# Expert weights inside the activations: the third feed-forward of a four-layer kernel, groups 1 to 3

## The chip, the cores and the metric

The kernel runs on one core of a Trainium2 chip. The metric is the device time of one execution in microseconds (us). Three runs of the kernel before took 1149.76, 1147.95 and 1148.5 us, so the median is 1148.5 us.

The core has engines that work side by side, each with its own queue that is worked off in order: TensorE (PE in the profile, with PEld for its weight loads), VectorE (DVE), ScalarE (ACT), GpSimd (POOL), and SyncE (SP), which here does nothing but issue DMAs.

## The reference

Four layers, each a cross-attention over 77 context positions and a feed-forward, run over 2 x 1024 tokens of width 256, all in fp32. The part that matters is the feed-forward of the third layer, a mixture of eight experts:

```
x = x + ffn(layernorm(x))

logits = xn @ gate_weight.T                  # 8 experts
scores = sigmoid(logits)
choice = scores + bias                       # pairs of experts form 4 groups:
                                             # keep the 2 groups with the largest sums,
                                             # then the 2 experts with the largest choice
w      = scores of the 2 experts kept, divided by (their sum + 1e-20)
y[t]   = sum over kept experts e of
         w[t, e] * ( silu(xn[t] @ gate_e.T) * (xn[t] @ up_e.T) ) @ down_e.T
```

A weight that multiplies a whole token's row can be applied to the expert's output (256 numbers) or to its hidden activations (128 numbers) alike, since the down projection is linear.

## The kernel before

The 2048 tokens lie in SBUF as four groups (`g`) of four sub-tiles (`j`) of 128 tokens. All eight experts are computed for every token; an expert that isn't chosen has weight 0.

The third feed-forward is `layer2_ffn` (L700 to L770; layers count from 0). It has three pieces:

- `route(g)` (L709 to L734) normalizes a group, transposes it to `xnT` (feature on the partition), makes the router's logits on TensorE, and on DVE the sigmoid, the choice of groups and experts (`top_mask`, L206 to L216, which compares every pair of values) and the weights `cw`, a tile of 128 tokens x 4 sub-tiles x 8 experts.
- `hidden(g, e)` (L736 to L751) makes one expert's hidden activations for the group's 512 tokens: four matmuls of 128x512 (L745) into two PSUM banks `pgu`, Silu on ACT (L750), the product with the up half on DVE (L751). The result `hT` has the expert's 128 hidden features on the partitions and tokens along the free axis.
- `down(g, j)` (L753 to L768) makes, for one sub-tile, eight matmuls of 128x256 (L758), each expert into its own quarter of two PSUM tiles `po`, and then eight multiply-adds on DVE (L765), `x = po * cw[:, j, e] + x`. Here tokens lie on the partitions, so the weight is one number per partition.

PSUM tiles come from helpers: `pbig` (L81, two tiles of two banks, used by `pgu`, by `po` and by most large products), `pone` (L86, one bank, three tiles in turn), `pside` (L94, one bank).

The driver (L1374 to L1416) works one group after the other: eight `hidden`, then four `down`. Between the pieces it puts work of other layers: the pieces of `chain` (the second layer's feed-forward and the third layer's attention, L554 to L690, for group g + 2), pieces of the last layer's set-up (`setup`, L795 to L882: products `pw` at L870, written to DRAM as `vd`), and `route(g + 1)`. Before that, `beside` (L1379) runs the chain of groups 0 and 1 next to the second layer's attention.

The written order isn't what the engines run: the framework's planner (switched on at L1489) simulates the program, reorders the instructions of each engine by its own estimates, and fixes the queues before the run.

After the stage comes `layer3_attention` (L884): it takes the SBUF that the closed pools leave, loads rope tables `cs` (L888), values `vw` (L897) and, for every sub-tile, a bias `rb` (L920, 616 KB), to which POOL adds a mask (L924), and makes queries `pq` on TensorE (L930) that DVE and POOL rotate (L781 to L791).

Of the kernel before, what the change touches and what calls it, by code (L numbers as in the profile page):

```python
# [22 lines left out]
F32 = mybir.dt.float32  # L23
# [4 lines left out]
AF = mybir.ActivationFunctionType  # L28
ALU = mybir.AluOpType
# [4 lines left out]
P = 128  # L34
D = 256
KC = D // P
NB, S = 2, 1024
NT = NB * S
G, J = 4, 4
GT = P * J  # L40
# [3 lines left out]
E = 8  # L44
CAP = 320
HID = 1024
INTER = 128
# [19 lines left out]
def tile_layers(ctx: ExitStack, tc: tile.TileContext, a: dict, out: bass.AP):  # L67
    nc = tc.nc
# [5 lines left out]
    st = ctx.enter_context(tc.tile_pool(name="st", bufs=3))  # L74
# [3 lines left out]
    dp = ctx.enter_context(tc.tile_pool(name="dram", bufs=1, space=DRAM))  # L78
    ps2 = ctx.enter_context(tc.tile_pool(name="ps2", bufs=2, space=PSUM))

    def pbig(name):  # L81
        return ps2.tile([P, 2, 512], F32, tag="p2", name=name)
# [3 lines left out]
    def pone(name):  # L86
        turn[0] += 1
        pool, tag = ((ps1, "p1"), (pst, "pt"))[turn[0] % 2]
        return pool.tile([P, 512], F32, tag=tag, name=name)
# [4 lines left out]
    def pside(name):  # L94
        return psr.tile([P, 512], F32, tag="pr", name=name)
# [7 lines left out]
    ident = cst[:, C_ID : C_ID + P]  # L103

    tokens = [xp.tile([P, J, ROW], F32, name=f"x{g}") for g in range(G)]
    xs = [t[:, :, :D] for t in tokens]
# [21 lines left out]
    def rowvec(name, n=D, parts=P):  # L128

        t = cp.tile([parts, n], F32, name=f"r_{name}")  # L130
        nc.sync.dma_start(t, a[name].partition_broadcast(parts))
        return t

    def weight(shape, name):
        return wp.tile(shape, F32, tag="w", name=name)
# [95 lines left out]
    def bc(v, n):  # L231

        return v.unsqueeze(len(v.shape)).to_broadcast([*v.shape, n])
# [62 lines left out]
    def attention(lay, weights, mask, deep=5, beside=None):  # L296
# [4 lines left out]
        with tc.tile_pool(name=f"at_{lay}", bufs=2) as ap:  # L301
# [175 lines left out]
            if beside:  # L477
                stages.append(beside)
# [210 lines left out]

        return prepare, scores, weighed, weights_turned, values, add  # L690

    def layer2_ffn_weights():
        wgu = []
        for nm in ("gate2T", "up2T"):
            t = weight([P, KC, E * INTER], nm)
            nc.sync.dma_start(t, a[nm].rearrange("(c p) n -> p c n", p=P))
            wgu.append(t)
        return wgu

    def layer2_ffn(fp, wgu):  # L700

        wd = weight([P, E, D], "down2T")
        nc.sync.dma_start(wd, a["down2T"].rearrange("e i h -> i e h"))
        gw = cp.tile([P, KC, E], F32, name="gw2")
        nc.sync.dma_start(gw, a["router2T"].rearrange("(c p) e -> p c e", p=P))
        gb = rowvec("L2_ffn_e_score_correction_bias", E)
        xnTs, cws, hTs = {}, {}, {}

        def route(g):  # L709
            n = f"f2{g}"  # L710
            xnTs[g] = xnT = normed(g, n, "f2")
            pl = small_logits(xnT, gw, n)

            sc = st.tile([P, J, E], F32, tag="sc", name=f"sc_{n}")
            nc.scalar.activation(sc, pl, AF.Exp, scale=-1.0)
            nc.vector.tensor_scalar(sc, sc, 1.0, None, ALU.add)
            nc.vector.reciprocal(sc, sc)
            ch = st.tile([P, J, E], F32, tag="ch", name=f"ch_{n}")
            nc.vector.tensor_tensor(
                ch, sc, gb.unsqueeze(1).to_broadcast([P, J, E]), ALU.add  # L720
            )
            pairs = ch.rearrange("p j (q i) -> p j q i", i=2)
            gs = st.tile([P, J, 4], F32, tag="gs", name=f"gs_{n}")
            nc.vector.tensor_tensor(gs, pairs[:, :, :, 0], pairs[:, :, :, 1], ALU.add)
            gm = top_mask(gs, 4, 2, f"{n}g")
            nc.vector.tensor_tensor(pairs, pairs, bc(gm, 2), ALU.mult)
            keep = top_mask(ch, E, 2, n)
            cws[g] = cw = st.tile([P, J, E], F32, tag="cw", name=f"cw_{n}")
            nc.vector.tensor_tensor(cw, sc, keep, ALU.mult)
            tot = st.tile([P, J], F32, tag="tot", name=f"tot_{n}")  # L730
            nc.vector.tensor_reduce(tot, cw, AX.X, ALU.add)
            nc.vector.tensor_scalar(tot, tot, 1e-20, None, ALU.add)
            nc.vector.reciprocal(tot, tot)
            nc.vector.tensor_tensor(cw, cw, bc(tot, E), ALU.mult)  # L734

        def hidden(g, e):  # L736
            n = f"f2{g}"
            if e % 4 == 0:
                hTs[g, e // 4] = fp.tile(
                    [P, E // 2, GT], F32, tag="hT", name=f"hT_{n}{e}", bufs=3  # L740
                )
            pgu = pbig(f"pgu_{n}{e}")
            for i in range(2):
                for kc in range(KC):
                    nc.tensor.matmul(  # L745
                        pgu[:, i, :], wgu[i][:, kc, e * INTER : (e + 1) * INTER],
                        xnTs[g][:, kc, :], start=(kc == 0), stop=(kc == KC - 1),
                    )
            sg = fp.tile([P, GT], F32, tag="sg", name=f"sg_{n}{e}")
            nc.scalar.activation(sg, pgu[:, 0, :], AF.Silu)  # L750
            nc.vector.tensor_tensor(hTs[g, e // 4][:, e % 4, :], sg, pgu[:, 1, :], ALU.mult)  # L751

        def down(g, j):  # L753
            x = xs[g][:, j, :]
            for half in range(2):
                po = pbig(f"po_f2{g}{j}{half}")
                for e in range(4):
                    nc.tensor.matmul(  # L758
                        po[:, e // 2, (e % 2) * D : (e % 2) * D + D],
                        hTs[g, half][:, e, j * P : (j + 1) * P], wd[:, 4 * half + e, :],  # L760
                        start=True, stop=True,
                    )
                for e in range(4):
                    ee = 4 * half + e
                    nc.vector.scalar_tensor_tensor(  # L765
                        x, po[:, e // 2, (e % 2) * D : (e % 2) * D + D],
                        cws[g][:, j, ee : ee + 1], x, ALU.mult, ALU.add,
                    )  # L768

        return route, hidden, down  # L770


    KV = 4
# [586 lines left out]
    with tc.tile_pool(name="masks", bufs=1) as mp:  # L1360
        mask0 = mp.tile([P, G, J * L], a["mask0"].dtype, name="mask0")
        mask1, mask2 = (
            mp.tile([P, G, J * L], a[f"mask{i}"].dtype, tag="mask", name=f"mask{i}")
            for i in (1, 2)
        )
        mb0, mb1 = (
            mp.tile([P, G, J * L], BF16, tag="mb", name=f"mb{i}") for i in range(2)
        )
        ctxn = mp.tile([L, NB, D], F32, name="ctxn")
        nc.sync.dma_start(ctxn, a["ctxn"].rearrange("b k d -> k b d"))  # L1370
        layer0_attention()
        with tc.tile_pool(name="none", bufs=1) as np0:
            layer0_ffn(np0)
        with (  # L1374
            tc.tile_pool(name="q8", bufs=1) as qp, tc.tile_pool(name="a2", bufs=1) as ap2,
        ):
            chain = []

            def beside(it):  # L1379


                if it == 0:
                    chain.extend((*layer1_ffn(qp, *quantized), *layer2_attention(ctxn, ap2)))
                for g in range(2):
                    k = it - (g + 1) * J + 1
                    if 0 <= k < len(chain):
                        chain[k](g)

            weights = attention_weights(
                "a1", ["L1_xattn_wq", "L1_xattn_wk", "L1_xattn_wv", "L1_xattn_wo"],  # L1390
                "L1_xattn_bo",
            )
            setup = layer3_setup()
            next(setup)
            quantized = layer1_ffn_setup()
            next(setup)
            gate_up = layer2_ffn_weights()
            layer1_attention(weights, beside)
            with tc.tile_pool(name="a3s", bufs=2) as sp, tc.tile_pool(name="f2", bufs=2) as fp:
                route, hidden, down = layer2_ffn(fp, gate_up)  # L1400
                setup.send(sp)


                route(0)
                for g in range(G):
                    pieces = [lambda e=e: hidden(g, e) for e in range(E)]
                    pieces += [lambda j=j: down(g, j) for j in range(J)]
                    for k, piece in enumerate(pieces):
                        if g + 2 < G and k < len(chain):
                            chain[k](g + 2)  # L1410
                        piece()
                        if g < 2 and k % 2 == 1 and k > 4 or (g, k) in ((0, 1), (0, 3)):
                            next(setup)
                        if g + 1 < G and k == E:
                            route(g + 1)
                made3 = next(setup)  # L1416
    route, experts = layer3_ffn()
# [75 lines left out]
```

## Time and profile before

| | |
|---|---|
| median of three runs | 1148.5 us |
| the profiled execution | 1150.59 us |
| its span (first to last instruction) | 1148.7 us |
| TensorE busy | 1029.8 us (90%) |
| VectorE busy | 719.4 us (63%) |
| GpSimd busy | 386.3 us (34%) |
| ScalarE busy | 362.1 us (32%) |
| mean granted TensorE clock | 0.952 |
| the chain that ended last | PE 56%, DVE 24%, DMA 7%, ACT 4%, issue 4%, POOL 4% |

A row of a group of instructions reads: source line, engine, operation, output <- inputs, shapes, how often | busy us, mean ns of one | idle us of that engine just before them, and what ended most of it. So a row with a high mean tells what a thing costs, and the part after the second bar tells whether its engine had to stand still for it. A row of the timeline reads: start us, length us, engine, line, operation, with idle time in square brackets. TensorE's matmuls are pipelined, so lengths of groups of them overlap a little.

Four gate and up matmuls with their four partners (one expert) take 3.43 us of TensorE, the eight down matmuls of one sub-tile 1.73 us when nothing holds them; one DVE multiply-add takes 0.48 us.

### The profile page before, as it was taken

The page shows a single profiled execution, that of the slowest core. Times are in us where ns is not written, and L with a number is a line of the kernel's source. Part 1 is how long each engine was busy: PE and PEld are TensorE (multiplying, and loading weights), DVE is VectorE, ACT ScalarE, POOL GpSimd, SP SyncE. Part 2 cuts the span into 40 slices and gives each one's busy share as a digit, 9 for nine tenths or more (in the row PEclk, how much of TensorE's full clock was granted, in tenths as well). Part 3 has the DMA queues.
Part 4 walks back from the last instruction along what each step waited for, and adds up shares of the span by engine and source line. Part 5 has one row for each costly group of instructions (what it writes and reads, how often), then busy time and mean ns, then how long its engine had stood idle before and what let it go on. Part 6 is the DMA issues. An engine that isn't in the chain of part 4 may idle for free.

```text
span 1148.7 us, 13916 instructions
## 1 busy us (share of the span) xinstructions
PE 1029.8 (90%) x4770; PEld 645.5 (56%) x4770; DVE 719.4 (63%) x1848; ACT 362.1 (32%) x1115; POOL 386.3 (34%) x368
## 2 busy tenths in 40 slices
PE   5499999999998987897998999899899958999996
PEld 3255554444444444455655546577678844766774
DVE  5567965776578898949586547677878731222211
ACT  1457640000076563131231110555355521111100
POOL 5443320112343544423120000675566641121211
PEclk9699998999999898898999999999999987999998
DMA  8400008245200000111102004523042323253630
GB/s 269 57 3 1 1 23 165 38 82 88 80 1 1 1 1 1 39 48 31 40 23 59 1 1 161 145 45 67 23 103 51 90 83 96 77 165 101 200 131 17
DMA packets 100279, 74.89 MB, mean 65 GB/s; under 512 B 57916, under 2 KB 90476, under 8 KB 100206
## 3 DMA queue, kind: packets, MB, share of 16 engines
q1 hardware_dynamic: 92974, 58.20, 18.3%
q10 hardware_dynamic: 4800, 9.46, 4.8%
q0 software_dynamic: 2432, 6.31, 1.6%
q8 instruction: 40, 0.66, 0.2%
q14 instruction: 33, 0.27, 0.1%
HBM read 55.35 MB, written 19.64 MB: 65 GB/s over the span
## 4 chain that ended last, share of the span: by engine, by line
PE 56%; DVE 24%; DMA 7%; ACT 4%; issue 4%; POOL 4%; SPq 0%; POOLq 0%; DVEq 0%; ACTq 0%
PE pe_f L545 10%; PE pgu_f L745 8%; PE poe_e L1273 4%; PE ph_e L1253 4%; PE po_a L1007 4%; DMA out_x<-ye_e,ids_e 3%; PE pq_a L930 3%; DVE x L765 3%; PE pc_a L450 3%; DVE x L156 2%; PE po_f L758 2%; PE pPT_a L437 2%; DVE mx_a L410 2%; DMA xe_e<-buf 2%; DVE sm_a L417 2%
## 5 line engine op out<-in xcount | busy, mean ns | idle before, releaser
L412 ACT ACTIVATE s_a<-psc_a,mx_a 128x77 f32<-128x77 f32 x512 | 121.5, 337 | 58.5 <-DVE mx_a L410 52.1
L419 POOL TENSOR_TENSOR s_a<-s_a,sm_a 128x616 f32<-128x616 f32 x64 | 78.3, 1223 | 123.9 <-DVE sm_a L418 89.4
L545 PE MATMUL pe_f<-ew,xnT_f 128*128 128x512 f32 x256 | 117.1, 607 | 0.0
L551 DVE SCALAR_TENSOR_TENSOR x<-pe_f,gate_f,x 128x256 f32<-128x256 f32 x128 | 61.8, 483 | 43.3 <-PE pe_f L545 40.7
L981 ACT ACTIVATE s_a<-s_a,mx_a 128x77 f32<-128x77 f32 x256 | 67.2, 347 | 61.4 <-DVE mx_a L979 61.2
L545 PEld LDWEIGHTS pe_f<-ew,xnT_f 128*128 128x128 f32 x256 | 48.3, 195 | 55.0 <-issue 53.0
L1007 PE MATMUL po_a<-vw,PT_a 128*128 128x256 f32 (+1 forms) x320 | 77.3, 381 | 0.8 <-ACT PT_a L1002 0.8
L1253 PE MATMUL ph_e<-xT_e,w 128*128 128x320 f32 x256 | 75.6, 436 | 0.0
L758 PE MATMUL po_f<-down2T,hT_f 128*128 128x256 f32 x256 | 65.0, 400 | 8.8 <-DVE x L765 8.7
L437 PE MATMUL pPT_a<-cst,s_a 128*128 128x128 f32 (+1 forms) x320 | 55.0, 292 | 17.8 <-POOL vr_a L343 11.5
L410 DVE TENSOR_REDUCE mx_a<-psc_a 128x4 f32<-128x308 f32 x128 | 57.9, 466 | 18.6 <-PE psc_a L401 11.4
L1077 DVE TENSOR_SCALAR hT_e<-ph_e,b1c 128x320 f32<-128x320 f32 (+1 forms) x36 | 20.6, 572 | 75.3 <-PE ph_e L1253 75.3
L930 PE MATMUL pq_a<-wq,xnT_a 128*128 128x512 f32 x128 | 60.5, 610 | 4.7 <-DVE s_a L972 4.7
L745 PE MATMUL pgu_f<-xnT_f,gate2T 128*128 128x512 f32 x128 | 63.5, 619 | 1.0 <-DVE hT_f L751 0.6
L765 DVE SCALAR_TENSOR_TENSOR x<-po_f,cw_f,x 128x256 f32<-128x256 f32 x128 | 60.8, 480 | 5.7 <-PE po_f L758 2.5
L437 PEld LDWEIGHTS pPT_a<-cst,s_a 128*128 128x128 f32 (+1 forms) x320 | 35.9, 143 | 49.5 <-issue 17.9
L1007 PEld LDWEIGHTS po_a<-vw,PT_a 128*128 128x128 f32 (+1 forms) x320 | 57.8, 190 | 9.6 <-issue 1.4
L1075 ACT ACTIVATE hT_e<-ph_e,b1c 128x320 f32<-128x320 f32 (+1 forms) x36 | 19.6, 545 | 138.0 <-PE ph_e L1253 138.0
L1273 PE MATMUL poe_e<-w,hT_e 128*128 128x256 f32 x256 | 61.3, 381 | 0.0
L758 PEld LDWEIGHTS po_f<-down2T,hT_f 128*128 128x128 f32 x256 | 48.3, 197 | 22.7 <-DVE x L765 15.4
L450 PE MATMUL pc_a<-PT_a,vblk_a 128*32 128x256 f32 (+1 forms) x512 | 57.2, 400 | 4.2 <-DVE PT_a L445 2.2
L745 PE MATMUL pgu_f<-xnT_f,up2T 128*128 128x512 f32 x128 | 60.1, 592 | 0.0
(311 smaller groups left out, 1979.8 us busy)
## 6 DMA issues: line engine op xcount, KB each, us to landing
w<-in_L_ffn_w SPq DMA_DIRECT2D x16, 1024.0 KB
rb_a<-in_relbias SPq DMA_DIRECT2D x16, 616.0 KB
buf<-none ACTq DMA_DIRECT2D x12, 769.5 KB
vd<-vo SPq DMA_DIRECT2D x8, 308.0 KB
vw<-vd SPq DMA_DIRECT2D x2, 1152.0 KB
xe_e<-buf SPq DMA_DIRECT2D x8, 257.0 KB
x<-in_x SPq DMA_DIRECT2D x4, 512.0 KB
ew<-in_L_ffn_expert_w SPq DMA_DIRECT2D x4, 512.0 KB
```

The lines of the kernel that those rows point to most:

```text
L410: nc.vector.tensor_reduce(mx, sv, AX.X, ALU.min)
L412: nc.scalar.activation(s[:, c, 4 * i + h, :], sv[:, h, :], AF.Exp, bias=mx[:, h : h + 1], scale=-1.0,)
L437: nc.tensor.transpose(pt[: wide(m), m - m0, k * P : (k + 1) * P], sp[k][:, c, m * P : m * P + wide(m)], ident,)
L450: nc.tensor.matmul(pc[cols, c, :], vblk[g // 2][: wide(m), c, m, cols], t[: wide(m), m, :], start=(k == 0), stop=(k == 1),)
L545: nc.tensor.matmul(pe[:, i, :], xnT[:, kc, j * P : (j + 1) * P], ew[half][:, kc, i * 512 : (i + 1) * 512], start=(kc == 0), stop=(kc == KC ...
L745: nc.tensor.matmul(pgu[:, i, :], wgu[i][:, kc, e * INTER : (e + 1) * INTER], xnTs[g][:, kc, :], start=(kc == 0), stop=(kc == KC - 1),)
L758: nc.tensor.matmul(po[:, e // 2, (e % 2) * D : (e % 2) * D + D], hTs[g, half][:, e, j * P : (j + 1) * P], wd[:, 4 * half + e, :], start=Tr ...
L765: nc.vector.scalar_tensor_tensor(x, po[:, e // 2, (e % 2) * D : (e % 2) * D + D], cws[g][:, j, ee : ee + 1], x, ALU.mult, ALU.add,)
L930: nc.tensor.matmul(pq[:, i, :], xnTs[g][:, kc, j * P : (j + 1) * P], wq[:, kc, i * 512 : (i + 1) * 512], start=(kc == 0), stop=(kc == KC - 1),
L1007: nc.tensor.matmul(po, t[:w, m, :], vws[g // 2][:w, m, :], start=(m == 0), stop=(m == NC3 - 1))
L1253: nc.tensor.matmul(ph[:, h % 2, :rows], w1[:, kc, h * P : (h + 1) * P], xT[:, kc, :], start=(kc == 0), stop=(kc == KC - 1),)
L1273: nc.tensor.matmul(po, hT[:, h, i * P : (i + 1) * P], w2[:, h, :], start=(h == 0), stop=(h == NH - 1),)
```

## The change

For groups 1 to 3 the weights are applied to the hidden activations instead of to the outputs. There the features lie on the partitions, so a weight has to be the same on all 128 partitions and differ along the free axis. `route(g)` therefore transposes `cw` (four transposes on TensorE into one `pside` tile, a copy on ACT) and writes the 8 x 512 numbers to DRAM (16 KB). `hidden(g, 0)` reads them back in eight DMAs, one per expert, each spreading one row of 512 numbers over all 128 partitions (256 KB, tag `cb`, eight buffers). In `hidden`, POOL multiplies Silu's result by `cb` before DVE multiplies it with the up half. In `down`, the eight matmuls of a sub-tile add up in one PSUM bank (`pone` instead of `pbig`), and one DVE add brings the sum to x. Group 0 keeps the old way.

So that the weights of the router are at hand earlier, `layer2_ffn()` is called before the second layer's attention, and `route(0)` stands at the end of `beside` instead of ahead of the group loop. `hidden` and `down` come from `units(fp)`, inside the pool.

The edits to `route`, `hidden` and `down`, and the driver:

```diff
-            cws[g] = cw = st.tile([P, J, E], F32, tag="cw", name=f"cw_{n}")
+            cw = st.tile([P, J, E], F32, tag="cw", name=f"cw_{n}")
...
             nc.vector.tensor_tensor(cw, cw, bc(tot, E), ALU.mult)
+            if g == 0:
+                cws[g] = cw
+                return
+
+            pc = pside(f"pcw_{n}")[:E, :]
+            for j in range(J):
+                nc.tensor.transpose(pc[:, j * P : (j + 1) * P], cw[:, j, :], ident)
+            cwT = st.tile([E, J, P], F32, tag="gT", name=f"cwT_{n}", bufs=2)
+            cwT = cwT.rearrange("e j p -> e (j p)")
+            nc.scalar.copy(cwT, pc)
+            cwds[g] = cwd = dp.tile([E, GT], F32, name=f"cwd_{n}")
+            nc.sync.dma_start(cwd, cwT)
...
+            def hidden(g, e):
+                n = f"f2{g}"
+                if e == 0 and g > 0:
+                    for i in range(E):
+                        cbs[i] = fp.tile([P, GT], F32, tag="cb", name=f"cb_{n}{i}", bufs=8)
+                        nc.sync.dma_start(cbs[i], cwds[g][i, :].partition_broadcast(P))
...
+                nc.scalar.activation(sg, pgu[:, 0, :], AF.Silu)
+                if g > 0:
+                    nc.gpsimd.tensor_tensor(sg, sg, cbs[e], ALU.mult)
+                nc.vector.tensor_tensor(hTs[g, e // 4][:, e % 4, :], sg, pgu[:, 1, :], ALU.mult)
...
+                po = pone(f"po_f2{g}{j}")[:, :D]
+                for e in range(E):
                     nc.tensor.matmul(
-                        pgu[:, i, :], wgu[i][:, kc, e * INTER : (e + 1) * INTER],
-                        xnTs[g][:, kc, :], start=(kc == 0), stop=(kc == KC - 1),
+                        po, hTs[g, e // 4][:, e % 4, j * P : (j + 1) * P], wd[:, e, :],
+                        start=(e == 0), stop=(e == E - 1),
                     )
...
+                nc.vector.tensor_tensor(x, x, po, ALU.add)
...
+                if it == J + len(chain):
+                    route(0)
...
-            gate_up = layer2_ffn_weights()
+            route, units = layer2_ffn()
             layer1_attention(weights, beside)
             with tc.tile_pool(name="a3s", bufs=2) as sp, tc.tile_pool(name="f2", bufs=2) as fp:
-                route, hidden, down = layer2_ffn(fp, gate_up)
+                hidden, down = units(fp)
                 setup.send(sp)
 
 
-                route(0)
                 for g in range(G):
```

More of the change, by code (lines that the diff above doesn't have):

```diff
@@ L690, in layer2_attention, with layer2_ffn @@
         return prepare, scores, weighed, weights_turned, values, add
-    def layer2_ffn_weights():
+    def layer2_ffn():
         wgu = []
@@ L697, in layer2_ffn_weights @@
             wgu.append(t)
[L698 to L703, printed above, removed]
         gw = cp.tile([P, KC, E], F32, name="gw2")
@@ L706, in layer2_ffn @@
         gb = rowvec("L2_ffn_e_score_correction_bias", E)
-        xnTs, cws, hTs = {}, {}, {}
+        xnTs, cws, cwds = {}, {}, {}
         def route(g):
@@ L734, in route @@
             nc.vector.tensor_tensor(cw, cw, bc(tot, E), ALU.mult)
[L736 to L744, printed above, removed]
+            if g == 0:
+                cws[g] = cw
+                return
+            pc = pside(f"pcw_{n}")[:E, :]
@@ new lines, in route, with units, down @@
+            for j in range(J):
[5 more added lines that the diff above has]
+            nc.sync.dma_start(cwd, cwT)
+        def units(fp):
+            wd = weight([P, E, D], "down2T")
+            nc.sync.dma_start(wd, a["down2T"].rearrange("e i h -> i e h"))
+            hTs, cbs = {}, {}
+            def hidden(g, e):
[4 more added lines that the diff above has]
+                        nc.sync.dma_start(cbs[i], cwds[g][i, :].partition_broadcast(P))
+                if e % 4 == 0:
+                    hTs[g, e // 4] = fp.tile(
+                        [P, E // 2, GT], F32, tag="hT", name=f"hT_{n}{e}", bufs=3
+                    )
+                pgu = pbig(f"pgu_{n}{e}")
+                for i in range(2):
+                    for kc in range(KC):
+                        nc.tensor.matmul(
+                            pgu[:, i, :], wgu[i][:, kc, e * INTER : (e + 1) * INTER],
+                            xnTs[g][:, kc, :], start=(kc == 0), stop=(kc == KC - 1),
+                        )
+                sg = fp.tile([P, GT], F32, tag="sg", name=f"sg_{n}{e}")
+                nc.scalar.activation(sg, pgu[:, 0, :], AF.Silu)
+                if g > 0:
+                    nc.gpsimd.tensor_tensor(sg, sg, cbs[e], ALU.mult)
+                nc.vector.tensor_tensor(hTs[g, e // 4][:, e % 4, :], sg, pgu[:, 1, :], ALU.mult)
+            def down(g, j):
+                x = xs[g][:, j, :]
+                if g == 0:
+                    for half in range(2):
+                        po = pbig(f"po_f2{g}{j}{half}")
+                        for e in range(4):
+                            nc.tensor.matmul(
+                                po[:, e // 2, (e % 2) * D : (e % 2) * D + D],
+                                hTs[g, half][:, e, j * P : (j + 1) * P], wd[:, 4 * half + e, :],
+                                start=True, stop=True,
+                            )
+                        for e in range(4):
+                            nc.vector.scalar_tensor_tensor(
+                                x, po[:, e // 2, (e % 2) * D : (e % 2) * D + D],
+                                cws[g][:, j, 4 * half + e : 4 * half + e + 1], x,
+                                ALU.mult, ALU.add,
+                            )
+                    return
+                po = pone(f"po_f2{g}{j}")[:, :D]
+                for e in range(E):
@@ L745, in hidden @@
                     nc.tensor.matmul(
-                        pgu[:, i, :], wgu[i][:, kc, e * INTER : (e + 1) * INTER],
-                        xnTs[g][:, kc, :], start=(kc == 0), stop=(kc == KC - 1),
-                    )
[L749 to L768, printed above, removed]
@@ L770, in layer2_ffn @@
-        return route, hidden, down
+                        po, hTs[g, e // 4][:, e % 4, j * P : (j + 1) * P], wd[:, e, :],
+                        start=(e == 0), stop=(e == E - 1),
+                    )
+                nc.vector.tensor_tensor(x, x, po, ALU.add)
+            return hidden, down
+        return route, units
     KV = 4
```

## The prediction

> **What bounds the kernel now.** I read the page first, then the busy time of each engine by stretch, then TensorE's waits in the third feed-forward, then the chain that leads out of it. The page's rows of busy time and of the costliest groups:
>
> ```profile
> PE 1029.8 (90%) x4770; PEld 645.5 (56%) x4770; DVE 719.4 (63%) x1848; ACT 362.1 (32%) x1115; POOL 386.3 (34%) x368
> ...
> L419 POOL TENSOR_TENSOR s_a<-s_a,sm_a 128x616 f32<-128x616 f32 x64 | 78.3, 1223 | 123.9 <-DVE sm_a L418 89.4
> ...
> L758 PE MATMUL po_f<-down2T,hT_f 128*128 128x256 f32 x256 | 65.0, 400 | 8.8 <-DVE x L765 8.7
> ...
> L745 PE MATMUL pgu_f<-xnT_f,gate2T 128*128 128x512 f32 x128 | 63.5, 619 | 1.0 <-DVE hT_f L751 0.6
> L765 DVE SCALAR_TENSOR_TENSOR x<-po_f,cw_f,x 128x256 f32<-128x256 f32 x128 | 60.8, 480 | 5.7 <-PE po_f L758 2.5
> ```
>
> TensorE is the bound. All down matmuls together waited 8.8 us, nearly all for the DVE multiply-adds of L765. So removing 96 of the 128 multiply-adds frees 46 us of VectorE (96 x 0.480), but only a few us of TensorE waits. By stretch (columns: from:to, length, busy PE, PEld, DVE, ACT, POOL with counts, then clock, DMA share, GB/s):
>
> ```profile
> 594.00:620.00 26.00, 23.04 (x111) 17.56 (x111) 24.55 (x87) 4.33 (x7) 0.37 (x1) 1.00 0.08 25
> ...
> 647.00:664.20 17.20, 16.12 (x72) 12.06 (x71) 15.42 (x36) 0.89 (x2) 0.00 (x0) 1.00 0.00 0
> 664.20:691.90 27.70, 27.70 (x65) 12.39 (x66) 8.65 (x17) 4.18 (x7) 1.26 (x2) 1.00 0.02 2
> 691.90:709.10 17.20, 16.30 (x73) 12.30 (x72) 14.58 (x31) 1.07 (x2) 0.00 (x0) 1.00 0.33 120
> ```
>
> These are the down phases of groups 1, 2 and 3, and group 3's gate and up phase (third row), where TensorE never rests. A down phase is paced by VectorE, a gate phase by TensorE alone.
>
> **How the stage ends.** The SP queue, its wait, and the chain of waits around the last down matmul:
>
> ```profile
> 709.07 0.88 SPq L888 DMA_DIRECT2D cs<-in_ropeq  x2
> ...
> SPq L888 <- PE po_f L758: 15.8, 1, 15.8
> ...
> 707.04 1.99 PE po_f L758 x8
> 709.04 3.67 PE pq_a L930 x8
> ...
> 724.70 2.58 POOL rb_a L924
> 727.28 0.02 issue
> 727.30 0.81 DVE s_a L972
> 728.11 0.04 issue
> 728.16 5.41 PE pq_a L930 x8
> ```
>
> The fourth layer's tables take the memory of the closed pool, so SP holds `cs`, then `vw` and `rb`, until the last down matmul ends. Call that time T (709.04). Issued at 709.07, they land at 724.66, T + 15.6, and the fourth layer's scores start from there. What the change does to the kernel is therefore what it does to T; the compiled program keeps that wait on the last down matmul.
>
> **Part 1: what is the same up to 550.3.** Moving `route(0)` into `beside` leaves each engine's instruction order as it was until the first group's new transposes; only the `gw2` and bias DMAs stand two or three places earlier on SP, ahead of nothing late. Cost 0. The window to predict is 550.3 to 709.04, 158.7 us.
>
> **Part 2: the most that can be won.** TensorE's work in that window, each bunch at its unstalled length from the timeline: 24 experts' gate and up x 3.433 = 82.4; 25 down sub-tiles x 1.733 = 43.3 (one of them group 0's last); 11 sets of four transposes x 0.44 = 4.8; five `pw` x 1.88 = 9.4; layer 2's scores, transposes and products 1.75 + 0.44 + 2.1; router logits 2 x 1.68 = 3.4. Sum 147.6. So the waits are 158.7 - 147.6 = 11.1 us: an accumulating down phase (12 DVE adds of about 0.45 instead of 96 multiply-adds) could win that at most.
>
> **Part 3: what TensorE gets more of before T.** The transposes of `cw`: 3 x 0.44 = 1.3 (the row is L175's 128x128 transposes). And in the changed order two of layer 3's `pq_a` bunches, 3.45 each, stand ahead of group 3's last down sub-tile, because the planner now has room there: 6.9. They are work that stood after T and was done in the shadow of the 15.6 us; ahead of T they are not hidden. Best case: 147.6 + 1.3 + 6.9 = 155.8, T = 706.1, a gain of 2.9.
>
> **Part 4: the way through DRAM.** `cw` of group 1 is ready on DVE at 548.8. Copy (about 0.6, as L179's 128x512), write, and read back: an earlier pair of this kind on SP (`vd_a` written 281.98, read issued 284.77) took 2.8, and its read landed 2.2 later. So the first `cb` is there near 556.7; it is needed when expert 0's Silu ends, near 561.7. The others, 256 KB each, come 0.7 to 0.8 apart at the 320 to 385 GB/s of this kernel's large loads, and are needed 3.4 apart. Hidden, with 5 us to spare; without it each late us is a TensorE us. On SP, `vd`, `w` and `ow2` DMAs queue behind; `w_0` (2 MB, 6.3 us) is still issued 15 us before T. Cost 0.
>
> **Part 5: a longer way to each hT.** The POOL multiply of 128x512 with two SBUF inputs: from L419 (616 columns, 1.22 us) and L630 (256 columns, about 0.7), about 1.1. From the last gate matmul: 0.2 + 0.60 (Silu) + 1.15 + 0.69 (L751) = 2.7 us, against 3.43 until the PSUM bank is wanted again. On an idle POOL it fits; the down matmuls interleaved between experts give more room. Here the Trainium skill speaks against the change: "GPSIMD Engine Reference", section 4.1, tells to keep two-input elementwise work off GpSimd, about half as fast as VectorE there; section 3.1 has 4497 ns for 2048 columns, an estimate of 1.1 us for 512. Row and rule agree on the price; at 2.7 against 3.43 the slowness itself costs nothing.
>
> **Part 6: where POOL is not idle.** Same page, section 1: GpSimd shares its SBUF interface with VectorE, and contends with DVE instructions that have two SBUF inputs. This trace shows it, as POOL and then DVE stand at 471:
>
> ```profile
> 471.43 2.40 POOL L685 TENSOR_TENSOR o_a<-o_a,r_L_xattn_gamma 128x1024 f32<-128x1024 f32 x1 [2.08 <-DVE o_a L156]
> 473.91 2.17 POOL L688 TENSOR_TENSOR x<-x,o_a 128x1024 f32<-128x1024 f32 x1
> ...
> 471.53 2.33 DVE L211 TENSOR_TENSOR eq_f20g<-gs_f 128x16 f32<-128x16 f32 x1
> ...
> 473.96 2.16 DVE L210 TENSOR_TENSOR gt_f20g<-gs_f 128x16 f32<-128x16 f32 x1
> ...
> 476.12 0.67 DVE L751 TENSOR_TENSOR hT_f<-sg_f,pgu_f 128x512 f32<-128x512 f32 x1
> ```
>
> Operations of 0.16 us take 2.3 and 2.2: each is held to the end of the POOL instruction, and in the gap between two POOL instructions two or three pass. L765 and L751 (one input in PSUM) are not held.
>
> In group 1 POOL must do, in this order: gamma (2.35), expert 4's multiply (1.1), the residual add (2.17), expert 5's multiply (1.1): from about 582.5 to 589.5 with hardly a gap. On DVE, ahead of `hT` of expert 4, stands group 2's selection (`ch` and twelve comparisons, two SBUF inputs each, some 3.1 us unheld). Held, it ends two us or so after POOL, and `hT` of expert 4 at about 592.4; unheld at about 587. My replay of TensorE's order: four experts to 571.4 and 580.5, six down products, expert 5 to 586.5, four down products to 588.2, then `pw`, which needs the bank that this `hT` frees. It stands 588.2 to 592.4: 4.2 us (bounds: 0 if unheld, 5 if more is held).
>
> A TensorE pause of this length has a second price:
>
> ```profile
> 539.45 3.70 PE L758 MATMUL po_f<-down2T,hT_f 128*128 128x256 f32 x13
> 547.11 3.20 PE L758 MATMUL po_f<-down2T,hT_f 128*128 128x256 f32 x8 [3.96 <-DVE x L765]
> ```
>
> After 3.96 us idle, eight down matmuls took 3.20 instead of 1.73, and the pause cost about 1.9 more with what follows at half clock. By "TensorE: Matmul & The Clock Gate", Part 1, the clock drops only after a window of about 3.4 us without work, and takes as long to return: an idle of 4.2 need not hold such a window whole, so 0 to 1.9. I take the row, which is as long: 1.6. T = 706.1 + 4.2 + 1.6 = 711.9, 2.9 later.
>
> **Groups 2 and 3.** POOL has only the experts' multiplies and short `rstd` powers; `hT` of expert 2, behind group 3's selection, comes 15.9 us after the group starts and is wanted at 17.6. Cost 0; margin 1.7 us, which is the next thing to go if POOL holds DVE longer there. Against all this, the second `pq_a` after the pause at 724 may run at full clock, as TensorE has less left to idle over: it took 5.41 instead of 3.45, so up to 1.9 back; I count 0.4, as the work left after T' still ends near T' + 17.
>
> **The sum.** +2.9 - 0.4 = +2.5. The profiled execution took 1150.6 at a span of 1148.7; the three runs shown have median 1148.5, 2.1 below it. The change is taken as the same on both: 1148.5 + 2.5 = **1151.0**. About 0.2%, 2.3 us, is what a measurement can tell here: 1146.2 to 1150.8 is "same".
>
> **Rivals.** (a) *No pause at `pw`*: the planner's order meets POOL earlier or later than my replay, and the selection passes before gamma starts, or in the gaps. For it: my replay's margin is a few us over a way of 40. Against it: gamma is released by the very DVE operations (L156) that stand directly ahead of the selection. T' = 706.1 to 707, time 1145.6 to 1146.5: faster. This is the other side; it decides when `hT` of expert 4 ends before 588.2. (b) *A short pause*, 1 to 3 us, no clock loss: T' 707 to 709, time 1146.5 to 1148.7: no change. (c) *More pauses*: POOL's 24 multiplies hold DVE also in groups 2 and 3 past the 1.7 us, one more pause of 3 with its clock: 1151 + 4 = 1155. (d) *`cb` late by more than its 5 us*: about 1153 for 2 us late; nothing in the trace speaks for it but that no row has such a spread. (e) *The change frees nothing in the down phases* since accumulating in one bank makes each matmul wait: 12 x 8 such starts at 0.05 add 5: 1156; the layer's gate matmuls accumulate pairs at 592 ns each with no gap, against it.
>
> **Chances.** The forecast's pause 0.45 (1149.8 to 1152.3, 0.33 of it beyond the bound), (a) 0.25 (0.22 faster), (b) 0.16 (0.13 same, 0.03 faster), (c) 0.08, (d) and (e) 0.06. So faster 0.25, same 0.28, slower 0.47. Range: from (a)'s 1145 to (c)'s 1156; the forecast's own range is 1149.8 to 1152.3.
>
> **What would show it.** Right: a TensorE wait of about 4 us ahead of a `pw` near 588, released by `hT`; eight matmuls after it at half clock; comparisons on DVE of 1 to 2 us while POOL multiplies; no DVE wait ahead of down matmuls; `cs` issued at the last down matmul near 712, its `rb` 15.6 later. Wrong: TensorE's idle near 588 under 1 us, a `cb` that POOL waits for, or `cs` leaving before 708.

## The result and the profile after

The changed kernel took 1154.78 us (median; 1152.54 to 1155.96) beside 1149.31 us for the kernel before: a ratio of 1.0043, with a 95% interval of 1.0027 to 1.0058, so 0.27% to 0.58% slower. Beside the later experiments the same kernel gave 1.0037 (1.0026 to 1.0047). The profiled execution took 1155.76 us at a span of 1154.0, where before it was 1150.59 at 1148.7.

The page of the changed kernel, its rows that answer to those shown of before:

```profile
PE 1034.5 (90%) x4782; PEld 651.2 (56%) x4782; DVE 688.4 (60%) x1764; ACT 363.8 (32%) x1118; POOL 416.3 (36%) x392
...
L769 DVE TENSOR_TENSOR hT_f<-sg_f,pgu_f 128x512 f32<-128x512 f32 x32 | 21.8, 680 | 72.8 <-POOL sg_f L768 61.0
...
L761 PE MATMUL pgu_f<-xnT_f,gate2T 128*128 128x512 f32 x128 | 64.0, 623 | 0.0
...
L768 POOL TENSOR_TENSOR sg_f<-sg_f,cb_f 128x512 f32<-128x512 f32 x24 | 30.4, 1265 | 77.4 <-ACT sg_f L766 77.4
```

VectorE is 31 us less busy and GpSimd 30 us more. All of GpSimd's idle time before its multiplies ends with ScalarE's Silu and none with a `cb` transfer, so the way through DRAM is never waited for there. The stretches of the changed kernel (columns as before: length, busy PE, PEld, DVE, ACT, POOL, then clock, DMA share, GB/s):

```profile
547.00:594.00 47.00, 41.33 (x160) 26.07 (x160) 31.95 (x95) 12.63 (x20) 18.03 (x15) 0.96 0.20 68
594.00:620.00 26.00, 25.60 (x84) 15.02 (x84) 11.07 (x34) 3.99 (x7) 3.79 (x4) 0.82 0.34 106
620.00:650.00 30.00, 30.00 (x103) 17.57 (x102) 14.77 (x54) 6.90 (x10) 7.59 (x7) 1.00 0.20 58
650.00:715.00 65.00, 65.00 (x216) 38.96 (x215) 14.56 (x32) 7.52 (x13) 15.20 (x13) 1.00 0.20 65
```

From 620 to 715 TensorE never rests: the waits of the down phases of groups 2 and 3 are gone. But the second row has a clock of 0.82 (it was 1.00), and the first hides a pause. Read us by us (columns: length, busy PE, clock, DMA share, GB/s), the clock falls to half within the pause and is back ten us later:

```profile
593.00:594.00 1.00, 0.00 (x0) 0.63 0.00 0
594.00:595.00 1.00, 0.60 (x2) 0.50 0.00 0
...
602.00:603.00 1.00, 1.00 (x2) 0.50 0.09 16
603.00:604.00 1.00, 1.00 (x3) 0.75 0.00 0
```

TensorE's timeline there and at the end of the stage:

```profile
586.74 1.88 PE L761 MATMUL pgu_f<-xnT_f,up2T 128*128 128x512 f32 x4
588.46 1.89 PE L792 MATMUL po_f<-down2T,hT_f 128*128 128x256 f32 x8
594.40 3.69 PE L900 MATMUL pw<-wo,vT 64*77 64x256 f32 x8 [4.05 <-DVE hT_f L769]
598.02 2.07 PE L792 MATMUL po_f<-down2T,hT_f 128*128 128x256 f32 x4
...
710.38 3.60 PE L960 MATMUL pq_a<-wq,xnT_a 128*128 128x512 f32 x8
713.81 0.60 PE L175 MATMUL pxnT_a<-cst,x 128*128 128x128 f32 x4
714.25 3.62 PE L792 MATMUL po_f<-down2T,hT_f 128*128 128x256 f32 x16
724.42 6.36 PE L960 MATMUL pq_a<-wq,xnT_a 128*128 128x512 f32 x8 [6.55 <-DVE r_a L815]
```

The forecast pause stands at its place: 4.05 us ahead of a `pw`, until `hT` of expert 4. VectorE in that time, ahead of this `hT`:

```profile
584.35 2.29 DVE L216 TENSOR_SCALAR m_f22g<-rank_f22g 128x16 f32<-128x16 f32 x1
586.68 1.20 DVE L721 TENSOR_TENSOR ch_f<-ch_f,m_f22g 128x32 f32<-128x32 f32 x1
587.91 2.13 DVE L210 TENSOR_TENSOR gt_f<-ch_f 128x64 f32<-128x64 f32 x1
589.97 1.29 DVE L211 TENSOR_TENSOR eq_f<-ch_f 128x64 f32<-128x64 f32 x1
591.19 0.21 DVE L210 TENSOR_TENSOR gt_f<-ch_f 128x64 f32<-128x64 f32 x1
...
593.66 0.68 DVE L769 TENSOR_TENSOR hT_f<-sg_f,pgu_f 128x512 f32<-128x512 f32 x1
```

Four operations of about 0.2 us take 6.9 us together, one for each of four POOL instructions that follow each other from 584.27 (gamma 2.35, expert 4's multiply 1.26, residual 2.17, expert 5's multiply 1.25). The fifth, after POOL has ended, takes 0.21. At 717.90 SP issues `cs`: the last down matmul, T', is 8.8 us later than in the profile before. The next score stage begins 8.9 us later too (a query product at 737.09 instead of 728.16), but there the half clock that took it 5.41 us before is gone, and the span ends 5.3 us later.

### The profile page after: what moved, and what is told of

Its sections match the earlier page's. It is cut to its first block, busy times and chain, and to the rows that moved or that the text cites. A ratio compares the mean times of both kernels' runs of the same rounds, so it can differ in the third digit from the quotient of the medians.

```text
span 1154.0 us, 13950 instructions
## 1 busy us (share of the span) xinstructions
PE 1034.5 (90%) x4782; PEld 651.2 (56%) x4782; DVE 688.4 (60%) x1764; ACT 363.8 (32%) x1118; POOL 416.3 (36%) x392
## 4 chain that ended last, share of the span: by engine, by line
PE 59%; DVE 20%; DMA 8%; ACT 5%; POOL 4%; issue 3%; SPq 1%; POOLq 0%; ACTq 0%; DVEq 0%
PE pe_f L545 10%; PE pgu_f L761 8%; PE poe_e L1303 4%; PE po_a L1037 4%; DMA out_x<-ye_e,ids_e 3%; PE po_f L792 3%; PE ph_e L1283 3%; PE pc_a L450 3%; PE pq_a L960 3%; DMA xe_e<-buf 2%; PE pPT_a L437 2%; DVE x L156 2%; PE psc_a L401 2%; DVE mx_a L410 2%; PE pq_a L374 2%
## 5 line engine op out<-in xcount | busy, mean ns | idle before, releaser
L769 DVE TENSOR_TENSOR hT_f<-sg_f,pgu_f 128x512 f32<-128x512 f32 x32 | 21.8, 680 | 72.8 <-POOL sg_f L768 61.0
L768 POOL TENSOR_TENSOR sg_f<-sg_f,cb_f 128x512 f32<-128x512 f32 x24 | 30.4, 1265 | 77.4 <-ACT sg_f L766 77.4
L1283 PEld LDWEIGHTS ph_e<-xT_e,w 128*128 128x128 f32 x256 | 47.5, 190 | 18.8 <-issue 3.1
```

The costliest lines, as they stand in the source:

```text
L1283: nc.tensor.matmul(ph[:, h % 2, :rows], w1[:, kc, h * P : (h + 1) * P], xT[:, kc, :], start=(kc == 0), stop=(kc == KC - 1),)
```

## The experiments

Theory A: the loss is the pause in group 1 with its half clock, plus the two query products that stand ahead of the last down matmul; without them the change is a gain. Its rivals: the move of `route(0)` costs, the multiply is too slow or its data late, or the place of the query products doesn't matter. All kernels here compute the whole reference.

The table has each kernel's ratio to the kernel before, and from its profile the length of the window of the prediction (from the point near 550 where the orders part, the weights' transposes or, without them, the `pxnT_a` transposes, to the issue of `cs`, that is to the last down matmul). The start of the window differs by some 3 us between executions, so the length says more than the end; it still differs by 1.8 us between the two profiles of the changed kernel. Differences given in us beside ratios are the ratio's share of about 1151 us, not differences of medians.

| kernel | ratio (95%) | window, us |
|---|---|---|
| before | 1 | 550.10 to 709.07: 159.0 |
| changed | 1.0043 (1.0027 to 1.0058) | 551.43 to 717.90: 166.5 |
| e5, changed, again | 1.0037 (1.0026 to 1.0047) | 548.88 to 717.16: 168.3 |
| e1, move of route(0) alone | 0.9998 (0.9981 to 1.0015) | 550.12 to 708.85: 158.7 |
| e2, gamma and residual on DVE | 0.9985 (0.9973 to 0.9996) | 550.84 to 709.06: 158.2 |
| e3, group 3's sums in pbig | 0.9989 (0.9976 to 1.0001) | 549.26 to 708.43: 159.2 |
| e4, e2 and e3 | 0.9928 (0.9904 to 0.9952) | 551.39 to 702.43: 151.0 |
| e6, before, bias first | 0.9967 (0.9953 to 0.9982) | 549.54 to 708.15: 158.6 |
| e7, changed, bias first | 1.0026 (1.0016 to 1.0036) | 550.96 to 717.26: 166.3 |
| e8, e4 and bias first | 0.9875 (0.9853 to 0.9898) | 548.06 to 699.54: 151.5 |
| e9, before, gamma and residual on DVE | 0.9990 (0.9976 to 1.0005) | 549.23 to 707.10: 157.9 |
| e10, e9 and bias first | 0.9975 (0.9966 to 0.9984) | 548.40 to 706.75: 158.4 |
| e11, multiply on DVE | 0.9984 (0.9974 to 0.9993) | 550.46 to 708.45: 158.0 |
| e12, groups 2 and 3 only | 1.0011 (1.0003 to 1.0019) | 550.91 to 711.11: 160.2 |

**The move of route(0) alone.** The changed kernel with the old way in all groups (`g >= 0` in the place of `g == 0`).

> The kernel before with only the move of route(0) into beside and the earlier loads of the router's weights; the down phases as before in all groups. Theory A (the loss comes from a pause of TensorE in group 1, and from query products that stand ahead of the last down matmul): no change, within 0.2% of the kernel before, and the last down matmul of group 3 at 709 +- 1. Theory B (the move itself costs, the changed kernel reached the window 1.1 us later): 1 us or more slower, with the later start near 551.4.

Measured 0.9998, window 158.7. Theory A's side: the move costs nothing, and the 1.1 us by which the changed kernel's profile came later to the window is scatter between executions (the repeat came there earlier than before).

**Group 3's gamma and residual on VectorE.**

```diff
-            nc.gpsimd.tensor_tensor(
+            eng = nc.vector if g == 3 else nc.gpsimd
+            eng.tensor_tensor(
                 o, o, gamma.unsqueeze(1).to_broadcast([P, J, D]), ALU.mult
             )
-            nc.gpsimd.tensor_tensor(xs[g], xs[g], o, ALU.add)
+            eng.tensor_tensor(xs[g], xs[g], o, ALU.add)
```

> The changed kernel with the two 128x1024 operations of group 3's second-layer attention (times gamma, added to x) on DVE instead of POOL. Theory A: with POOL free, the selection on DVE isn't held, hT of expert 4 comes before 588, the pause of 4.05 us and the half clock behind it (4.5 us) go; the last down matmul ends near 709.5 instead of 717.9, and the kernel is 6 to 8.5 us faster than the changed one: 1146 to 1149, ratio to before about 0.999. Theory B (the pause only moves, since POOL's multiply or the copy of the weights is late anyway): last down matmul still after 714, 1153 or more.

VectorE's timeline in this kernel, the same operations:

```profile
584.34 1.21 DVE L686 TENSOR_TENSOR o_a<-o_a,r_L_xattn_gamma 128x1024 f32<-128x1024 f32 x1
585.47 0.16 DVE L216 TENSOR_SCALAR m_f22g<-rank_f22g 128x16 f32<-128x16 f32 x1
585.58 1.22 DVE L689 TENSOR_TENSOR x<-x,o_a 128x1024 f32<-128x1024 f32 x1
586.73 0.68 DVE L770 TENSOR_TENSOR hT_f<-sg_f,pgu_f 128x512 f32<-128x512 f32 x1
587.32 0.18 DVE L722 TENSOR_TENSOR ch_f<-ch_f,m_f22g 128x32 f32<-128x32 f32 x1
...
588.74 0.21 DVE L210 TENSOR_TENSOR gt_f<-ch_f 128x64 f32<-128x64 f32 x1
588.87 0.22 DVE L211 TENSOR_TENSOR eq_f<-ch_f 128x64 f32<-128x64 f32 x1
```

The four operations take 0.16 + 0.18 + 0.21 + 0.22 = 0.77 us instead of 6.9. The pause is gone (TensorE goes from the down products to `pw` at 589.43 without a wait), and the clock from 594 to 604 is 1.00. The window is 8.3 us shorter, 4.05 of pause and about 4.5 of half clock; the time is 0.5% below the changed kernel's (1.0037 to 0.9985, 6.0 us). The planner here also put `hT` of expert 4 ahead of the comparisons, so the kernel alone doesn't part holding from order. The durations do: in the changed kernel's own order, 6.9 - 0.77 = 6.1 us less would have brought `hT` to about 588.2, ahead of the end of TensorE's work at 590.3.

**Group 3's down sums in pbig.**

```diff
-                po = pone(f"po_f2{g}{j}")[:, :D]
+                po = pbig(f"po_f2{g}{j}")[:, 0, :D] if g == 3 else pone(f"po_f2{g}{j}")[:, :D]
```

> The changed kernel with the down sums of group 3 in the tiles of pbig instead of pone: the planner then puts group 3's down matmuls after its gate matmuls and all query products after them. The pause in group 1 stays. Theory A: the last down matmul ends 5 to 7 us earlier (711 to 713, two query products of 3.45 less, up to 1.5 for the last hT that is no longer covered), tables and scores follow it, and the kernel is 3 to 5 us faster than the changed one: 1150 to 1152. Rival (where the query products stand is all the same, since they must be made anyway): 1154 to 1155.

The order of TensorE and GpSimd up to group 3 is that of the changed kernel, and the pause is there again (4.05 us). All three query products now follow the last down matmul; the window is 7.3 us shorter, about the two products' 6.9. The time fell by 0.48% (5.5 us), a little more than expected. Where these products stand does matter.

**Both.**

> Both edits of the last two kernels. Theory A: last down matmul near 703 to 704, 5 us before that of the kernel before; 1143 to 1146, ratio 0.995 to 0.998. If the two costs are not independent: 1147 or more.

Window 151.0: 15.5 us less than the changed kernel's 166.5, nearly the sum of 8.3 and 7.3. Time 0.9928, below what was expected. The two causes are independent, and together they are the whole loss and more (e4 rests on 6 runs and e8, below, on 5, so their intervals are wider).

**Tables of the fourth layer in another order.** The first two `rb` loads are issued ahead of the `vw` loads.

```diff
+            first = {it: load_bias(it) for it in range(2)}
             vws = []
...
-                rb = ap.tile([P, H, L], F32, tag="rb", name=f"rb_{n}")
-                nc.sync.dma_start(
...
+                rb = load_bias(it) if it > 1 else first.pop(it)
```

> The kernel before with one change: the first two bias loads rb (616 KB each) are issued ahead of the values vw (2 x 1.2 MB), behind cs as before. Theory A (the wait for the last down matmul sets the fourth layer through the 15.6 us to the landing of rb): rb lands near T + 6, the first masked scores start 4 to 6 us earlier, and the kernel is 3 to 6 us faster than before, ratio 0.995 to 0.997. Rival (rb only seemed to be waited for; the rotation of the queries or vw ends as late): within 0.2%.

0.9967, 3.8 us faster with the same window: the 15.6 us from the last down matmul to `rb` did set the start of the fourth layer. (The first masked scores start 15.2 us after the issue of `cs` instead of 18.2, so 3.0 us earlier where 4 to 6 were expected.)

> The changed kernel with the same order of loads. If the two are independent, as much faster than the changed kernel as the previous one is than before: 3 to 6 us, ratio to before 0.998 to 1.001. If the query products that stand ahead of the last down matmul leave less to wait for: 5 us or more, since cs is no longer followed by 2.4 MB when the third query product needs its tile back.

A miss: only 1.2 us below the changed kernel (1.0026 against 1.0037, whose intervals meet). The timelines of SP, of TensorE and of VectorE in this kernel bear on why:

```profile
717.26 0.88 SPq L918 DMA_DIRECT2D cs<-in_ropeq  x2
718.19 2.83 SPq L928 DMA_DIRECT2D rb_a<-in_relbias  x2
```

```profile
723.94 6.25 PE L967 MATMUL pq_a<-wq,xnT_a 128*128 128x512 f32 x8 [6.71 <-DVE r_a L815]
730.03 1.04 PE L986 MATMUL pqT_a3t<-cst,q_a 128*128 128x128 f32 x8
```

```profile
720.33 2.36 DVE L811 TENSOR_TENSOR q_a<-pq_a,cs 128x1024 f32<-128x1024 f32 x2 [2.64 <-DMA cs<-in_ropeq]
...
733.44 0.79 DVE L1009 SCALAR_TENSOR_TENSOR s_a<-psc_a,rb_a 128x616 f32<-128x616 f32 x1
```

Two query products ahead of T' fill both tiles of `pbig` and can't be rotated before `cs` is there. The third waits 6.71 us for a tile and runs at half clock (6.25 instead of 3.45). POOL has the first rotated query ready at 726.4, 9.1 us after `cs` is issued, but its transposes stand behind that product until 730.03, and the first scores get their bias at 733.44: 16.2 us after the issue of `cs`, where it was 18.3 in the changed kernel. In e6 the same step is at 15.2 us, from 18.2, and the next query product there loses its half clock too (3.70 instead of 5.41), a gain that the changed kernel already had. So the third product takes part of what the order of loads gives; how much of the 2.6 us between e6's gain and e7's it is, intervals of this width don't tell.

> The combination of the two edits (group 3's gamma and residual on DVE, group 3's sums in pbig) and the order of loads. Independent: 10 to 13 us faster than before, ratio 0.988 to 0.991. Not independent: about 8, as the combination alone, 0.993.

0.9875, 14.4 us faster than before, and the best kernel of this study: its median is 1138.55 us beside 1151.76, 13.2 apart. With the query products back behind the last down matmul, the order of loads pays 0.5% (0.9928 to 0.9875).

**The same edits without the change.**

> The kernel before with group 3's gamma and residual on DVE. There TensorE stood 0.62 us for a product near 585 that was held behind them. Theory A (the gain of this edit in the changed kernel was the pause that the change had made): 0 to 1 us, within 0.2% of before. Rival (moving them to DVE is good by itself, whatever the down phases do): 3 us or more faster, as in the changed kernel.

> The kernel before with group 3's gamma and residual on DVE and the first bias loads ahead of the values: all that the best version has, without the weights inside the activations. If the change itself is worth what the replay says once its pause and its query products are out of the way (some 5 to 6 us): ratio to before 0.995 to 0.998, against 0.9875 with it. Rival (the best version's gain is that of the other two edits): below 0.992.

0.9990 and 0.9975: the intervals of e9 and of before meet, and e10 is 2.9 us faster than before, where e8 is 14.4. So the best kernel's gain is not that of its other edits. Weights inside the activations, with group 3's sums in `pbig`, are worth 0.9875/0.9975, 1.0% or 11.5 us there; between e9 and e4, without the order of loads, it is 7.2 us. Why the two differ was not followed up. My estimate of 5 to 6 us was too low.

**The multiply on VectorE.**

```diff
-                    nc.gpsimd.tensor_tensor(sg, sg, cbs[e], ALU.mult)
+                    nc.vector.tensor_tensor(sg, sg, cbs[e], ALU.mult)
```

> The changed kernel with the multiply by the weights on DVE instead of POOL; gamma and residual stay on POOL. Theory A (what held the selection was a nearly unbroken row of four POOL instructions, two of them the change's own): the pause in group 1 shrinks to 0 to 2 us, 1147 to 1152 where the changed kernel has 1156. Rival (gamma and residual alone hold as long, or the extra 24 multiplies fill DVE): pause of 4 us or more, no faster than the changed kernel.

0.9984, and TensorE's longest wait in group 1 after the weights are copied is 0.18 us. The new multiply takes 0.68 on VectorE (once 2.45, held by the residual on POOL), against 1.27 on GpSimd. One word moved undoes the pause, as well as e2's move does. The planner's order differs here too (the selection is done before gamma starts), so this run shows that the pair of old and new work on POOL is needed for the pause, not which of the two holds more.

**Groups 2 and 3 only.** `g < 2` in the place of `g == 0`.

> The new way for groups 2 and 3 only; group 1 keeps its multiply-adds. Theory A: no pause of 4 us in group 1, the waits of group 1's down phase stay (some 4 us), groups 2 and 3 lose theirs (some 6 us) and two query products stand ahead of the last down matmul (6.9): last down matmul 708 to 712, time within 0.3% of before. Rival (the slower time comes from groups 2 and 3): 1155 or more, as the changed kernel.

1.0011, window 160.2: group 1 has its old waits (0.62, 0.95 and 1.61 us, and no pause of 4 us), groups 2 and 3 none, and the two query products stand ahead of the last down matmul. This is Theory A's side.

## Why the prediction was right, and where its sizes were off

The forecast was 1151.0, 0.2% slower, with a range of 1145 to 1156 and a chance of 0.47 for slower. The measured 1154.8 is slower, in the range, but above the forecast's own 1149.8 to 1152.3.

- *Part 1, the move costs nothing*: right (e1).
- *Parts 2 and 3, the waits to be won and the query products to be paid*: right. Groups 2 and 3 run without a TensorE wait, and e3 puts the price of the products' place at 7.3 us of window, where 6.9 was reckoned. The window of e4, which has neither the pause nor these products, is 151.0, where the two parts give 147.6 + 1.3 = 148.9.
- *Part 4, the way through DRAM*: hidden, as forecast. Not forecast was that TensorE waits for the copy of the weights: 0.66 us at 553 in the profile after, ahead of a `pxnT_a` transpose, and as much in each kernel where group 1 has the new way.
- *Part 5, the multiply*: 1.27 us, 1.1 was taken; no wait from it by itself. The rule of the Trainium skill's "GPSIMD Engine Reference", section 4.1, held as to price (0.68 against 1.27), and e11 shows it was worth following here. By the timelines of VectorE the reason is that of its section 1, the hold on VectorE, rather than the length of the multiply.
- *Part 6, the pause*: right in place, releaser and size, 4.05 for 4.2 (one operation passed in each gap between GpSimd's instructions, not two or three). The term that was mis-sized is what it costs afterwards: "0 to 1.9 ... I take the row, which is as long: 1.6". It was about 4.5. The clock, read us by us, was 0.50 from about 593.3 to 603.5 in the changed kernel, and TensorE was busy from 594.40 on: 9.1 us at half clock lose 4.5. The row that I took (3.96 us idle at 543) was followed by only 3.4 us at 0.50. One row was not enough to take a price from.
- *The sum at the end of the window*: forecast 711.9, measured 717.9. The half clock took 2.9 more than reckoned, the window began 1.1 later, and around the weights' transposes 1.3 were lost (the wait of 0.66 for the copy, and the transposes at half clock, 1.03 instead of 0.44). That is 5.3 of the 6.0; the rest is spread.
- *What is given back after T'*: "up to 1.9 back; I count 0.4". 3.5 us came back by the end (8.8 later at T', 5.3 at the end of the span): 1.7 as the query product at 737 runs at full clock (3.70 us instead of 5.41), the rest further on in the fourth layer; where, was not followed up. The third query product was reckoned as hidden; it waited 6.55 us and ran at half clock, and in e7 it stands on the way to the first scores.

The trace of before held a closer row for Part 6, ten us earlier than the one taken: a `pw` that waited about as long for VectorE.

```profile
533.15 3.69 PE L870 MATMUL pw<-wo,vT 64*77 64x256 f32 x8 [4.63 <-DVE x L765]
```

There the clock was 0.50 from 530.7 to 540.9, and TensorE was busy for 7.1 us of that, a loss of about 3.6 us. With that row the forecast would have been about 2 us higher.

So two errors of 3 to 6 us stood against each other, and the net came out 2 to 3 us low. The mechanism was foreseen; that the time came no further from the forecast, and stayed in the range, owes something to luck, since the two errors cancel in part and neither was reckoned at its size. Of the rivals, (a) is what e2 and e11 show once POOL is free; (b), (c) with its pauses in groups 2 and 3, (d) and (e) didn't happen.

## What to carry to other kernels

Work given to an idle engine is paid for where that engine isn't idle: list what already stands in its queue at each point, and what on the other engine is held meanwhile. When a faster stage lets the planner pull later work forward, look for what waits for the end of the stage: here 6.9 us of products, free behind it, were not free ahead of it. A change whose main mechanism works can still lose; undoing its two side effects turned 0.4% slower into 0.7% faster, and 1.2% with a better order of loads (1.0% of it the change's own, by e8 against e10).

## What the runs showed of the hardware that was not expected

- The half clock after a pause lasts for very different times, and the length of the pause doesn't set them. Worked out from the mean clock of short stretches, it was 3.4 us after 2.32 us idle (548.8 to 552.3 in the profile after) and after 3.96 us idle (547.7 to 551.1 in the profile before); 6.8 us after 3.61 us idle (547.9 to 554.7 in the repeat, e5) and after 6.55 us idle (723.0 to 729.8 in the profile after); and 10.2 us after the pause of 4.05 us, in the changed kernel, its repeat, e3 and e7 alike, with TensorE busy all but the first 1.1 to 1.6 us of it. After the pause of 4.6 us ahead of the `pw` near 533 it was 10.2 us in the profile before and 13.6 in the profile after, with the same instructions behind it. These are one, two, three and four times 3.4. "TensorE: Matmul & The Clock Gate", Part 1, in the Trainium skill, counts in windows of about 3.4 us, which agrees; it has the half clock come after an idle window, where 2.32 us idle, less than such a window, were enough here, and the full clock back after one busy window, which the 9.1 us of work at half clock from 594.40 on contradict. What keeps the clock low so long there (`pw` products of 64 rows by 77 columns and single down matmuls run in that time) was not tested.
- VectorE's tensor_scalar with one SBUF input (L216, 128x16) was held 2.29 us while GpSimd worked, where it takes 0.16 in e2. So two SBUF inputs are not the only condition. The Trainium skill's "GPSIMD Engine Reference", section 1, also names VectorE's 2-port performance modes; whether L216 runs in one, no run here shows.
